# Preparing a last attention layer early, during another layer's context steps, and keeping it in DRAM

## The chip, the cores and the metric

The kernel runs on one core of a Trainium2 chip. A core has TensorE (PE, with its weight loads PEld), VectorE (DVE), ScalarE (ACT), GpSimd (POOL) and SyncE (SP, which here only issues DMAs), each with a queue of its own that is worked off in order. Data lie in SBUF (128 partitions) and PSUM, and in DRAM. The metric is the device time of one execution in microseconds (us), as the median of several runs.

## The reference

Four transformer blocks in a row change `x` (8 batch elements, 256 tokens, 320 channels, float32), with a context of 120 rows by 192 channels per batch element:

- Layer 0: self-attention, cross-attention to the context, both with 20 heads and with queries, keys, values and softmax weights rounded to 8-bit steps, then a gated feed-forward.
- Layer 1: self-attention, cross-attention, gated feed-forward, unquantised.
- Layer 2: cross-attention to 104 text rows and 16 image rows, each with keys and values of its own.
- Layer 3, 8 heads, the layer that the change is about:

```python
enc, ca = encoder_hidden_states[:, :end_pos], encoder_hidden_states[:, end_pos:]   # 116 rows, 4 tokens
hs = _mha(hidden_states @ Wq, enc @ Wk, enc @ Wv)
ca_q1 = jnp.einsum('btc,th->bch', ca, Wq_ca)[:, indices, :]
ca_hs1 = _mha(ca_q1, residual, residual)
ca_hs2 = _mha(ca_hs1 @ Wq, ca @ Wk_ca, ca @ Wv_ca)
out = (hs + ca_hs2) @ Wout + b_out + residual
```

Three products in it depend on the context and the weights alone, not on `x`: `Wq_ca` spread over heads (`wz`), the token keys `ca @ Wk_ca` behind `Wq` (`wk2`), and the token values `ca @ Wv_ca` before `Wout` (`v2W`). Making these three is "the preparation".

## The kernel before, in words

`x` stays in SBUF throughout. The program text fixes the order of the work: Python generators yield after each piece, and two helpers interleave them.

- `weave(*parts)` runs rounds. In each round it takes one piece from every part whose start round has come. `paced(steps, idle)` makes a part give a piece only every `idle + 1` rounds.
- `run_flow(items)` runs layer 0's feed-forward and everything after it as a pipeline of items. An item has four generators: `project`, `tops` (row maxima of the scores), `out` (exponentials, values, output) and `fin`. In step `i` it takes turns among `tops` of item `i+1`, `project` of `i+2`, `fin` of `i-1` and `out` of `i`. Items 0 to 3 are layer 0's feed-forward, 4 to 11 and 12 to 19 layer 1's two attentions, 20 to 23 its feed-forward, then layer 2's eight attention items ("both") and layer 3's eight (`last_item`).

Layer 0's second attention (class `Quant`, object `c`) has two weaves. The first, the score loop, combines `tops_all` (scores and their maxima, L1309 and L1312), `sums_all` (exponentials L1360 and their sums L1375), the rounding of the operands (`whole_all`) and the values (`v`). It takes six rounds per batch element. The second, the output loop, is `out_all`: exponentials again, rounded weights (DVE, L1468), values (L1450), output projection (`project_out_steps`). It takes three rounds per batch element, 24, and four to drain.

Both weaves also carry `context_steps`: 29 pieces that compute the keys and values of the context for layers 1, 2 and 3 (matmuls L668 and L670), evict them with ACT into staging tiles (`kst`, one buffer; `vst`, two) and write them with SP's DMAs to DRAM, where the later items fetch them. One piece is taken ahead; 18 run in the score loop, one in three rounds; the other 10 in the output loop, one in two rounds. The staging and the context's weights lie in the pool `context`, on the right side of SBUF. When it closes, the pool of layer 0's second feed-forward weights (`w_ff2`) takes its place; the load of `ff2` (L96) waits for that.

`load_last` runs after step 23. It closes the feed-forward pools, opens `w_last` in their place and issues the loads of layer 2's output weights (40 DMAs, L275) and layer 3's weights: `lwk_ca`, `lwv_ca` (L96, L98), `lwq` (L776), `lwo` (L790), then `open_last` (L795 to L853). That one loads `sel` and `wq_ca`, fills `wz` and `ones`, and returns an item of its own, inserted at place 29 among layer 2's items:

- its `project`, `first`: three transposes of `wq_ca` (L815), multiplied by a head mask into `wz` (L817, L821); then `k2` and `v2T`, the token keys and values spread by head (12 matmuls each, L120, and three multiplications, L834);
- its `tops`, `second`: `wk2` = `WqT` times `k2` (18 matmuls, copies L845, L846) and `v2W` = `v2T` times `Wout` (12 matmuls, copy L851);
- its `out` and `fin` are empty.

`WqT` and `Wout` for it come through the pool `f_weights`, tag `o`, two buffers. SP issues DMAs in the program's order, so the small DMAs of `top_scores` that carry the row maxima `nT` into `qT` (L397) wait behind whatever SP was given earlier. `out` of the same item cannot start its score matmuls (L414) before these have landed. Layer 3's `last_item` reads `wz` and `wk2` in `project` (L890, L127) and `v2W` in `fin`.

Of the kernel before, what the change touches and what calls it, by code (L numbers as in the profile page):

```python
# [11 lines left out]
F32 = mybir.dt.float32  # L12
BF16 = mybir.dt.bfloat16
AF = mybir.ActivationFunctionType
ALU = mybir.AluOpType
# [3 lines left out]
P = 128  # L19
# [19 lines left out]
T3 = 4  # L39
# [15 lines left out]
class Kernel:  # L55
# [737 lines left out]
    def open_last(self, pool, w):  # L793

        nc = self.nc  # L795
        HT = H3 * T3
        w["pool"] = pool
        sel = w["sel"] = pool.tile([Q3, 2, N], F32, name="sel3")
        nc.sync.dma_start(sel, self.a["sel"].rearrange("(t p) n -> p t n", p=Q3))
        wq_ca = pool.tile([T3, C], F32, name="wq_ca")  # L800
        nc.sync.dma_start(wq_ca, self.a["L3_xattn_Wq_ca"])
        wz = w["z"] = pool.tile([P, 3, H3, PAD], F32, name="wz")
        nc.gpsimd.memset(wz, 0.0)
        ones = w["ones"] = pool.tile([P, PAD3], F32, name="ones3")
        nc.gpsimd.memset(ones, 1.0)
        k2, v2T = (self.work.tile([P, 3, B * HT], F32, tag="xh", name=n) for n in ("k2", "v2T"))
        wk2 = w["k2"] = pool.tile([P, 3, B * HT], F32, name="wk2")
        v2W = w["v2"] = pool.tile([P, B * HT // P, C], F32, name="v2W")
        pairs = lambda m: self.cols[:, COL_BMK + m * HT : COL_BMK + (m + 1) * HT]

        def first():

            ps = self.bank()
            for c, n in CH:
                nc.tensor.transpose(ps[:n, c * T3 : (c + 1) * T3], wq_ca[:, c * P : c * P + n], self.ident[:T3, :T3])  # L815
            for c, n in CH:
                nc.vector.tensor_tensor(  # L817
                    wz[:n, c, :, :T3], pairs(c)[:n].rearrange("p (h t) -> p h t", t=T3),
                    ps[:n, c * T3 : (c + 1) * T3].unsqueeze(1).to_broadcast([n, H3, T3]), ALU.mult,
                )  # L820
            nc.scalar.copy(wz[64:, 2], wz[:64, 2])  # L821
            yield

            rep = [self.ctxT[:n, c, :, K3:].unsqueeze(2).to_broadcast([n, B, H3, T3]) for c, n in CHC]
            for dst, wt in ((k2, w["wk_ca"]), (v2T, w["wv_ca"])):
                yield
                ps = self.pair()
                for m, rows in CH:
                    o = ps[:rows, m // 2, m % 2 * B * HT : (m % 2 + 1) * B * HT]
                    self.mm(  # L830
                        o.rearrange("p (b h t) -> p b h t", h=H3, t=T3),
                        [(wt[:n, c, m * P : m * P + rows], rep[c]) for c, n in CHC],
                    )
                    nc.vector.tensor_tensor(  # L834
                        dst[:rows, m].rearrange("p (b k) -> p b k", k=HT), o.rearrange("p (b k) -> p b k", k=HT),
                        pairs(m)[:rows].unsqueeze(1).to_broadcast([rows, B, HT]), ALU.mult,
                    )

        def second():

            ps = self.pair()
            for m, rows in CH:
                o = ps[:rows, m // 2, m % 2 * B * HT : (m % 2 + 1) * B * HT]
                self.mm(o, [(w["wqT"][:n, c, m * P : m * P + rows], k2[:n, c]) for c, n in CH])
                nc.scalar.copy(wk2[:rows, m, :], o)  # L845
            nc.scalar.copy(wk2[64:, 2, :], wk2[:64, 2, :])  # L846
            yield
            ps = self.pair()
            for i in range(B * HT // P):
                self.mm(ps[:, i, :C], [(v2T[:n, c, i * P : (i + 1) * P], w["wo_rows"][:n, c, :]) for c, n in CH])  # L850
            nc.scalar.copy(v2W, ps[:, :, :C])  # L851

        return first, second, lambda: iter(()), lambda: iter(())  # L853
# [652 lines left out]
def kernel(ctx: ExitStack, tc: tile.TileContext, a, out):  # L1506
    k = Kernel(ctx, tc, a, out)
    with ExitStack() as es:
# [15 lines left out]
        with tc.tile_pool(name="l0", bufs=1) as pool:  # L1524
# [17 lines left out]
            with tc.tile_pool(name="context", bufs=1, side="right") as cp:  # L1542
                k.open_context(cp, dram)
                ahead = k.context_steps()
                next(ahead)
                loaded["w"] = [k.weight_ff1(fp, "L0_xattn_Wff1")]
                brow["ff0"] = k.bias_row(k.fk, 2)
                w["self"], brow["self"] = load("L1", "q1", "k1", "v1", "o1_w", 3)
                c.steps()
                for _ in c.whole(0, True):  # L1550
                    pass
                n = len(c.units)
                k.weave(
                    (0, c.tops_all()), (n + 4, c.sums_all()), (0, c.whole_all()), (5, v),
                    (1, k.paced(islice(ahead, 18), 2)),
                )
                c.weight_steps()
                k.weave((0, c.out_all()), (0, k.paced(ahead, 1)))
# [16 lines left out]
        def load_last():  # L1575
# [3 lines left out]
            w3.update({f"w{n}": k.weight(pool, f"lw{n}", f"L3_xattn_W{n}") for n in ("k_ca", "v_ca")})  # L1579
            w3["wqT"] = k.weight(k.fw, "o", "L3_xattn_WqT", 2)  # L1580
# [93 lines left out]
```

## Time and profile before

| | us |
|---|---|
| median of 3 runs | 2303.44 |
| lowest, highest | 2302.2, 2305.42 |
| the profiled execution's own time | 2306.57 |
| span of its profile | 2304.7 |
| score loop of layer 0's second attention, about | 447 to 566 |
| its output loop, about | 585 to 691 |
| first and last matmul of the preparation's `first` and `second` | 1857.3 and 1902.6 |
| first matmul that reads `lwq` (layer 3's first item) | 1967.0 |

The profiled execution is one run with a hardware profiler; its own time is 1.87 us more than its span (what lies ahead of the first and behind the last instruction). Times in the text are counted from the start of that span. Where a line of the profile is labelled L120, it is the helper `mm`, whatever the matmul is for, and tiles tell these apart: the profile calls `wk2` and `k2` without their digits, `wk` and `k`, and the `WqT` and `Wout` tiles `o`. A row of the chain of waits gives its start, its length, and the engine, tile and line, with the number of instructions merged.

### The profile page before, as it was taken

Reading aid. Unit: us, or ns where it says so; the run is one execution under the profiler, and the core shown is the slowest. Engines: PE = TensorE matmul, PEld = TensorE weight load, DVE = VectorE, ACT = ScalarE, POOL = GpSimd, SP = SyncE. Lnnn points to the kernel's source line nnn. Section 1 sums busy time; section 2 is a strip of 40 time slices with the busy share of each in tenths; the row PEclk is TensorE's granted clock in tenths of the full one; section 3 lists DMA queues with packets and bytes.
Section 4 is the critical chain, followed back from the end, with each engine's and each line's share of the span. In section 5 each row is a group of like instructions: output and inputs, shape, how many; then the busy total and the mean of one; then the engine's idle time right before and its main releaser. Section 6 shows DMA issues by size and latency. Waiting matters only on the chain.

```text
span 2304.7 us, 38236 instructions
## 1 busy us (share of the span) xinstructions
PE 2104.4 (91%) x16413; PEld 1187.8 (52%) x16413; DVE 1117.6 (48%) x1691; ACT 823.0 (36%) x1248; POOL 360.3 (16%) x371
## 2 busy tenths in 40 slices
PE   7978878789789999999999999999999798999997
PEld 4643344544454455465555555454455455566664
DVE  4288666454761222236565666511122555555465
ACT  2347866357542121124444433310212222222221
POOL 1093055450520000000000010100001000001100
PEclk9989888799799999999999999999999899999999
DMA  4010000432220000020001101100000200000000
GB/s 113 14 14 2 1 1 1 116 104 65 54 74 4 0 1 0 1 89 2 2 2 27 38 24 41 34 1 0 1 1 14 54 24 13 19 21 23 26 17 17
DMA packets 78439, 60.99 MB, mean 26 GB/s; under 512 B 48314, under 2 KB 68222, under 8 KB 77758
## 3 DMA queue, kind: packets, MB, share of 16 engines
q1 hardware_dynamic: 74206, 54.83, 8.7%
q10 hardware_dynamic: 4064, 3.71, 0.5%
q8 instruction: 130, 2.13, 0.4%
q14 instruction: 39, 0.32, 0.0%
HBM read 41.49 MB, written 16.25 MB: 25 GB/s over the span
## 4 chain that ended last, share of the span: by engine, by line
PE 72%; DVE 15%; ACT 5%; issue 3%; POOL 2%; SPq 2%; DMA 1%; ACTq 0%; DVEq 0%; POOLq 0%
PE pf L564 13%; PE pf L120 12%; PE pf L127 9%; PE pa L120 7%; PE pa L431 6%; PE pf L414 4%; PE pf L568 4%; PE pf L129 3%; DVE negm L1312 3%; PE pf L369 2%; DVE rs L439 2%; PE pf L1353 2%; PE pa L1375 2%; PE pf L668 2%; DVE negm L376 2%
## 5 line engine op out<-in xcount | busy, mean ns | idle before, releaser
L564 PE MATMUL pf<-xTf,ff 128*128 128x512 f32 x640 | 294.9, 603 | 3.7 <-DVE negm L376 2.5
L420 ACT ACTIVATE e<-pf 128x1024 f32<-128x1024 f32 (+2 forms) x176 | 157.6, 944 | 231.5 <-PE pf L414 225.0
L376 DVE TENSOR_REDUCE negm<-pf 128x4 f32<-128x1024 f32 (+4 forms) x224 | 187.8, 885 | 104.4 <-PE pf L369 104.4
L439 DVE RECIPROCAL rs<-pa 128x256 f32<-128x256 f32 x88 | 152.3, 1745 | 143.9 <-PE pa L431 143.9
L573 DVE SCALAR_TENSOR_TENSOR hT<-pf,cols_sb,gl 128x512 f32<-128x512 f32 x80 | 60.1, 751 | 331.2 <-ACT gl L572 331.2
L564 PEld LDWEIGHTS pf<-xTf,ff 128*128 128x128 f32 x640 | 115.1, 190 | 161.8 <-issue 154.9
L461 POOL TENSOR_TENSOR xb<-x_sb,brow 128x640 f32<-128x640 f32 x40 | 62.0, 1550 | 825.9 <-DVE x_sb L467 782.2
L1360 ACT ACTIVATE e<-pf,sc_s 128x1024 f32<-128x1024 f32 x160 | 169.4, 1116 | 54.9 <-PE pf L1353 48.8
L1312 DVE TENSOR_REDUCE negm<-pf 128x4 f32<-128x1024 f32 (+2 forms) x128 | 143.4, 1132 | 64.6 <-PE pf L1309 58.3
L120 PE MATMUL pf<-ff,hT 128*128 128x320 f32 x640 | 174.4, 434 | 0.0
L572 ACT ACTIVATE gl<-pf,cols_sb 128x512 f32<-128x512 f32 x80 | 55.0, 687 | 305.0 <-PE pf L568 305.0
L414 PE MATMUL pf<-qT,kT 32*128 32x256 f32 (+1 forms) x1280 | 129.4, 415 | 24.6 <-DMA qT<-nT 16.0
L120 PEld LDWEIGHTS pf<-ff,hT 128*128 128x128 f32 x640 | 120.9, 190 | 55.5 <-issue 6.1
L369 PE MATMUL pf<-kT,qT 32*128 32x120 f32 (+1 forms) x1920 | 114.6, 334 | 17.3 <-ACT e L420 17.1
L120 PE MATMUL pa<-o,oT 128*128 128x320 f32 x352 | 109.8, 454 | 10.1 <-DVE oT L440 8.9
L369 PEld LDWEIGHTS pf<-kT,qT 32*128 32x128 f32 x1920 | 85.1, 194 | 55.2 <-ACT e L420 25.8
L581 POOL TENSOR_TENSOR xb<-x_sb,brow 128x640 f32<-128x640 f32 x16 | 25.1, 1570 | 559.4 <-DVE x_sb L586 543.8
L431 PE MATMUL pa<-e,v 128*32 128x256 f32 (+1 forms) x1280 | 108.4, 394 | 3.1 <-ACT e L420 1.7
L1353 PE MATMUL pf<-Q,K 32*128 32x256 bf16 (+1 forms) x960 | 86.7, 300 | 25.8 <-DVE negm L1312 17.6
L414 PEld LDWEIGHTS pf<-qT,kT 32*128 32x128 f32 (+1 forms) x1280 | 72.1, 185 | 73.2 <-issue 42.1
L1468 DVE TENSOR_SCALAR w<-e 128x1024 bf16<-128x1024 f32 (+2 forms) x128 | 87.1, 689 | 46.6 <-ACT e L1360 46.3
L127 PE MATMUL pf<-xT,q 128*128 128x256 f32 x384 | 102.3, 396 | 2.1 <-DVE hT L573 1.9
(279 smaller groups left out, 3371.3 us busy)
## 6 DMA issues: line engine op xcount, KB each, us to landing
ff<-in_L_xattn_Wff_dram SPq DMA_DIRECT2D x1, 2560.0 KB
qT<-nT SPq DMA_DIRECT2D x160, 4.0 KB
ff<-in_L_xattn_ff_w_dram SPq DMA_DIRECT2D x1, 2560.0 KB
out_dram<-x_sb SPq DMA_DIRECT2D x16, 160.0 KB
kd_cross<-kst SPq DMA_DIRECT2D x8, 300.0 KB
vd_cross<-vst SPq DMA_DIRECT2D x8, 300.0 KB
vd_both<-vst SPq DMA_DIRECT2D x8, 300.0 KB
kT<-kd_cross SPq DMA_DIRECT2D x8, 300.0 KB
```

Source lines behind the costliest of these rows:

```text
L120: self.nc.tensor.matmul(out, l, r, start=i == 0, stop=i == len(pairs) - 1)
L127: self.nc.tensor.matmul(o, *t[c], start=c == 0, stop=False)
L369: nc.tensor.matmul(s[j // 2][:, j % 2, o : o + nk], qT[r : r + PAD, g, t * P : (t + 1) * P], kT[r : r + PAD, g, :nk], start=True, stop=True,)
L376: nc.vector.tensor_reduce(negm[:, n, 2 * i : 2 * i + 2, g0 : g0 + len(gs), :].rearrange("p j g t -> p j (g t)"), sv[:, :, :, k0:k1], AX.X, ...
L414: nc.tensor.matmul(s[j // 2][:ks, j % 2, o : o + N], kT[r : r + PAD, g, c * ks : (c + 1) * ks], qT[r : r + PAD, g, :], start=True, stop=True,)
L420: nc.scalar.activation(e[:ks, 2 * i : 2 * i + 2, :n], s[i][:ks, :, :n], AF.Exp, scale=scale)
L431: nc.tensor.matmul(o[j * PAD : (j + 1) * PAD, what * N : (what + 1) * N], w, es[g][:ks, j, c * N : (c + 1) * N], start=first and c == 0 an ...
L439: nc.vector.reciprocal(rs, o[:, N:])
L564: nc.tensor.matmul(s[:, k, :], w1[:, c, col : col + P], xT[:, c, :], start=c == 0, stop=False)
L1312: nc.vector.tensor_reduce(negm[:, 2 * h : 2 * h + 2, gs[0] : gs[-1] + 1, :].rearrange("p j g t -> p j (g t)"), s[:, :, : len(gs) * TPB * n ...
L1353: nc.tensor.matmul(s[at // 2][:ks, at % 2, o : o + N], l, m, start=not shift and o == 0, stop=shift and o + N == n, skip_group_check=True,)
L1360: nc.scalar.activation(e[:ks, :, :n], ps[:ks, :, :n], AF.Exp, scale=self.sc[:ks, 9:10])
```

## The change

The preparation becomes a generator, `weights_last_steps`, that runs behind the last context step in the output loop. It has a pool of its own (`ahead_last`, opened where `context` was closed), loads its weights there, and writes `wz`, `wk2` and `v2W` to three DRAM tiles (384, 384 and 320 KB) from a staging tile. It yields five times with work between: `wz`, `k2`, `wk2`, `v2T`, `v2W`. The zero fill of `wz` is an ACT instruction there, in place of POOL's memset. `open_last` now loads the three from DRAM. The item at place 29 is gone, and so are the loads of `lwk_ca`, `lwv_ca`, `WqT` and `Wout` in `load_last`. The context steps are moved forward: 21 run in the score loop, one in two rounds, and the remaining 7 with the preparation in the output loop, again one in two rounds.

```diff
     def open_last(self, pool, w):
...
+        w["k2"] = pool.tile([P, 3, B * HT], F32, name="wk2")
+        w["v2"] = pool.tile([P, B * HT // P, C], F32, name="v2W")
+        w["z"] = pool.tile([P, 3, H3, PAD], F32, name="wz")
+        for n in ("z", "k2", "v2"):
+            nc.sync.dma_start(w[n], self.wd[n])
         sel = w["sel"] = pool.tile([Q3, 2, N], F32, name="sel3")
...
+    def weights_last_steps(self, pool, dram):
+        nc = self.nc
+        HT = H3 * T3
+        self.wd = {"z": dram.tile([P, 3, H3, PAD], F32, name="wd_z"),
+                   "k2": dram.tile([P, 3, B * HT], F32, name="wd_k2"),
+                   "v2": dram.tile([P, B * HT // P, C], F32, name="wd_v2")}
+        wq_ca = pool.tile([T3, C], F32, name="wq_ca")
+        nc.sync.dma_start(wq_ca, self.a["L3_xattn_Wq_ca"])
+        wca = {n: self.weight(pool, f"w{n}", f"L3_xattn_W{n}") for n in ("k_ca", "v_ca")}
+        big = lambda n: self.weight(pool, "big", n)
+        wt = big("L3_xattn_WqT")
+        staged = lambda n: pool.tile([P, 3, B * HT], F32, tag="staged", name=n)
+        heads = lambda n: pool.tile([P, 3, B * HT], F32, tag="heads", name=n)
...
+        wz = staged("wz_st").rearrange("p c (h r) -> p c h r", r=PAD)
+        zero = self.ident[:, :1].unsqueeze(2).to_broadcast([P, 3 * H3, PAD])
+        nc.scalar.activation(wz.rearrange("p c h r -> p (c h) r"), zero, AF.Identity, scale=0.0)
+        ps = self.pair()
...
+        nc.scalar.copy(wz[64:, 2], wz[:64, 2])
+        nc.sync.dma_start(self.wd["z"], wz)
+        yield
+        k2 = by_head(heads("k2"), wca["k_ca"])
+        yield
+        ps = self.pair()
+        st = staged("wk2_st")
+        for m, rows in CH:
+            o = ps[:rows, m // 2, m % 2 * B * HT : (m % 2 + 1) * B * HT]
+            self.mm(o, [(wt[:n, c, m * P : m * P + rows], k2[:n, c]) for c, n in CH])
+            nc.scalar.copy(st[:rows, m, :], o)
+        nc.scalar.copy(st[64:, 2, :], st[:64, 2, :])
+        nc.sync.dma_start(self.wd["k2"], st)
+        wt = big("L3_xattn_Wout")
+        yield
+        v2T = by_head(heads("v2T"), wca["v_ca"])
+        yield
+        ps = self.pair()
+        for i in range(B * HT // P):
+            self.mm(ps[:, i, :C], [(v2T[:n, c, i * P : (i + 1) * P], wt[:n, c, :]) for c, n in CH])
...
+        nc.scalar.copy(st, ps[:, :, :C])
+        nc.sync.dma_start(self.wd["v2"], st)
+        yield
...
-                    (1, k.paced(islice(ahead, 18), 2)),
+                (1, k.paced(islice(ahead, 21), 1)),
...
-                k.weave((0, c.out_all()), (0, k.paced(ahead, 1)))
+            def rest():
+                yield from ahead
+                context.close()
+                with tc.tile_pool(name="ahead_last", bufs=1, side="right") as pool:
+                    yield from k.weights_last_steps(pool, dram)
+
+            k.weave((0, c.out_all()), (0, k.paced(rest(), 1)))
...
-            w3.update({f"w{n}": k.weight(pool, f"lw{n}", f"L3_xattn_W{n}") for n in ("k_ca", "v_ca")})
-            w3["wqT"] = k.weight(k.fw, "o", "L3_xattn_WqT", 2)
-            w3["wo_rows"] = k.weight(k.fw, "o", "L3_xattn_Wout", 2)
...
-            w3["item"] = k.open_last(pool, w3)
+            k.open_last(pool, w3)
...
-        items.insert(29, lambda: w3["item"])
```

`by_head` holds the former matmuls and mask products of `k2` and `v2T` unchanged.

## The prediction

> **What bounds the kernel now.** I read the page first: TensorE is busy almost throughout and carries most of the chain that ended last, so an instruction taken off it counts unless something else is late behind it.
>
> ```profile
> span 2304.7 us, 38236 instructions
> ...
> PE 2104.4 (91%) x16413; PEld 1187.8 (52%) x16413; DVE 1117.6 (48%) x1691; ACT 823.0 (36%) x1248; POOL 360.3 (16%) x371
> ...
> PEclk9989888799799999999999999999999899999999
> ...
> PE 72%; DVE 15%; ACT 5%; issue 3%; POOL 2%; SPq 2%; DMA 1%; ACTq 0%; DVEq 0%; POOLq 0%
> ```
>
> To be seen: 91% busy, a granted clock that sags in places, 72% of the chain on PE. An average says nothing of a stage, so next come the two stages that the change touches. The late one is the run of steps in which layer 2's items meet the preparation item. I cut it where PE resumes `out` of a new item (first L414 of a step).
>
> ```profile
> core 0: us, PE busy (x) PEld busy (x) DVE busy (x) ACT busy (x) POOL busy (x), PEclk, DMA share, GB/s
> 1808.26:1834.28 26.02, 24.15 (x242) 15.26 (x242) 16.16 (x22) 8.41 (x14) 0.00 (x0) 0.84 0.17 48
> 1834.28:1864.18 29.90, 27.02 (x251) 16.16 (x251) 17.50 (x27) 7.60 (x12) 1.54 (x1) 0.89 0.11 28
> 1864.18:1897.51 33.33, 32.02 (x242) 16.86 (x242) 17.06 (x26) 8.48 (x15) 2.60 (x4) 1.00 0.07 21
> 1897.51:1938.27 40.76, 35.36 (x327) 21.74 (x327) 20.71 (x30) 11.63 (x21) 4.10 (x5) 1.00 0.06 17
> 1938.27:1963.66 25.39, 23.33 (x242) 14.52 (x242) 16.17 (x22) 8.41 (x14) 0.00 (x0) 0.87 0.06 17
> ```
>
> The columns are stretch, length, busy time of PE, PEld, DVE, ACT and POOL, then the granted clock and the DMA's share and GB/s. The first and the last row are ordinary steps: 26.02 and 25.39 us, mean 25.7. The three between are 29.90, 33.33 and 40.76 us, and PE is busy in nearly all of it. The last holds two steps, the second without any `out`. The chain of waits there:
>
> ```profile
> 1933.67 0.82 PE pf L314 x6
> ...
> 1936.44 1.58 DMA qT<-nT
> 1938.02 0.25 issue
> 1938.27 1.14 PE pf L414 x14
> ```
>
> PE finishes the next transposes at 1934.49 and does nothing until 1938.27, because the row maxima (`nT`) must still go through a DMA into `qT`, and no `out` covers that.
>
> The early stage is layer 0's second attention. It has two loops: the score loop (447 to 566 us, PE busy 106.2 of 119.0) and the output loop (585 to 691, PE busy 90.1 of 106.0). I cut them by batch element, by the times of DVE's L1312 and L1468:
>
> ```profile
> 536.90:549.20 12.30, 11.36 (x144) 5.64 (x145) 7.14 (x14) 8.36 (x14) 0.00 (x0) 1.00 0.20 51
> 644.00:660.70 16.70, 14.44 (x111) 8.86 (x110) 7.54 (x16) 8.25 (x14) 2.62 (x2) 0.95 0.15 57
> 660.70:671.90 11.20, 10.09 (x87) 6.08 (x85) 8.01 (x16) 6.77 (x10) 2.24 (x2) 1.00 0.17 50
> 671.90:680.30 8.40, 6.58 (x71) 3.75 (x70) 7.15 (x16) 5.39 (x6) 2.71 (x2) 0.98 0.56 190
> ```
>
> The first row is one batch element of the score loop with two context steps: PE 11.36 of 12.30 us. The other three are the output loop with two, one and no context step: 16.7, 11.2 and 8.4 us. So one context step of 3.2 us of PE (L668 and L670, 0.98+0.62+0.98+0.62 in the chain at 656 to 658) lengthens the loop by 2.8 to 4.15 us. These loops hide little PE work.
>
> **What is removed late.** PE's work of the preparation, from the chain: `k2` 1.25+1.25+1.15 = 3.65, `v2T` 1.26+1.25+1.15 = 3.66, `wk2` 1.69+1.63+1.58 = 4.90, `v2W` 4.01, three transposes 0.29; together 16.5 us. Its evictions (ACT 0.37x3, 0.40x2, 0.69; DVE 0.4x6, 0.18x3) lie beside PE. Its slot in the pipeline goes too: the step with no `out`. The five intervals sum to 155.4 us; five ordinary ones are 5 x 25.7 = 128.5. Gain **26.9**, of which 16.5 is work, 3.8 the wait on `nT`, and the rest (6.6) other gaps and the ten L120 matmuls at 1858.55 that take 5.63 us where ten take 2.89 elsewhere. Next late after this is the ordinary step itself; layer 3's items need `wz`, `wk2`, `v2W` over 100 us after they are loaded.
>
> **SP's queue in `load_last`.** PE idles 11.89 us until 1808.26 for `nT`, which SP issues from 1803.33 after all the weights; so each issue ahead of it is on the path. Removed: four `lwk_ca`/`lwv_ca` loads (1787.41 to 1789.65, 2.24 us) and `wq_ca` (0.44). Added: three loads from DRAM, each like `kT<-kd_both` (0.39 plus a gap of 0.1), 1.5 us. Net -1.2. Against it stands a rule: the Trainium skill, "DMA: Bandwidth & Descriptors", section on queues, rings and completion order, says that each DMA engine consumes a ring's descriptors in order. The three loads are 1.09 MB and stand right ahead of `nT`; at the 426 GB/s that the trace shows for `ff` at 984 to 988 us they take 2.6 us. If `nT` waits for all of it, the sum is +1.4; by the issue times alone -1.2. Part of the data moves while SP still issues, so I take **-0.5**, and keep -1.2 to +1.4. WqT and Wout leave SP at 1308.8 and 1480.2; the `nT` behind them were issued at 1319 or later anyway: nothing. The POOL memset of `wz` (0.74) precedes nothing urgent: nothing. If that cover failed it would cost its 0.74.
>
> **What is added early.** All of the preparation's PE work, 16.5 us, now stands among the last rounds of the output loop, one piece every second round; the context moves forward to make room: three steps (values of batch 7, L2's image keys, L3's first values) leave the output loop for the score loop. From the chain these are 1.27+0.73 = 2.0, 1.15+0.73+0.72+0.72 = 3.3 and 1.83+0.75 = 2.6: 7.9 us.
> - Output loop: +16.5 -7.9 = **+8.6**, at an exposure of 1 (2.8 to 4.15 for 3.2 in the rows above, i.e. 0.88 to 1.3). The fill of `wz_st` has no row; ACT's L744 fills 192 columns in 0.36 and L1360 moves 1024 in 1.1, so 768 lie between, about 0.9; ACT is busy about half of this loop (54.2 of 106), so nothing. If uncovered: 0.9 plus 2.6 of other evictions. The first load into the new pool must await the last context tiles' writes, then land; the transposes come two rounds (about 7 us) later, against a write of 4.5 and a load of some 2: nothing, at worst 2. The write-backs and `ff2`'s load shift by up to 20 us; `ff2` was issued at 670 and is first used at 740: nothing.
> - Score loop: +7.9 at PE's 92 to 96% busy. Also, a context step now comes every second round instead of every third. Each writes a staging tile that the next may not touch until its DMA has landed: `kst` has one buffer, `vst` two.
>
> ```profile
> 569.55 0.95 ACT vst L721 x2
> 570.51 0.02 issue
> 570.52 4.51 DMA vd_both<-vst
> ```
>
> This is such a wait: ACT may write `vst` again only 4.51 us after the last write's end. The rule: the same page, section "Anatomy of one DMA", puts a fixed part of about 2 us, mostly the receipt of the write, on top of bytes over 436 GB/s (fitted there to GpSimd's queue, while SP issues these); for 300 KB an estimate of 2.7 us. The trace says 4.51, and decides. At two rounds PE has 2.73 (a third of 8.2, an element's PE time without context steps: 12.3 less 2 x 2.0) plus 2.0 for values or 3.0 for keys: 4.8 or 5.7 us. The buffer's cycle is about 0.8+4.51+0.1 = 5.4 for the cross values, 2.3 of ACT (507.24 to 509.5) plus some 4 = 6.3 for keys. Excess 0.6 x 4 and 0.6 x 7, i.e. 6.6 by the row. By the rule the cycles are 3.6 and 5.0, and the excess is nil. With three PSUM pairs PE can run a little ahead of a waiting ACT. I take half the row, **+3.5**, between 0 and 10. Behind ACT's wait stand the `e` exponentials (L1360), and behind those PE's L1375 sums.
>
> **Sum.** -26.9 -0.5 +8.6 +7.9 +3.5 = **-7.4 us**. Against the profiled execution (2306.57 us, of which the span is 2304.7) that is 2299.2; it lies 3.1 above the median of the timed runs, 2303.44, so I forecast **2296.0**.
>
> **Rivals.**
> 1. *The loops hide it.* PE is idle 12.8 us in the score loop and 15.9 in the output loop; if half of the 24.4 us of moved and added work fell into it, early cost would be 20.0 - 12.2 = 7.8, total -19.6, 2283.8. For: the idle time is there, and the output loop's elements differ from 8.4 to 16.7 us. Against: the three rows above, where each step shows in full.
> 2. *It only changes place.* The dense pacing costs the full 10 instead of 3.5: total -0.9, 2302.5. For: ACT evicts `kst` on the chain already. Against: between values steps of L2 the two `vst` take turns, 9.6 us apart.
> 3. *Slower, by the staging buffers and the clock.* If each of the 21 dense steps waits 1.5 us and PE, idle in those waits, drops to half its clock (granted 0.50 from 448 to 460 us after a gap at 444 to 449, 0.59 from 585 to 605), the score loop pays 21 x 1.5 = 31.5 instead of 3.5: total +20.6, 2324. It turns slower, by more than a measurement tells from no change, from 3.5+7.4+4.6 = 15.5 us, 0.74 a step. Against: PE's share of 92 to 96% leaves it little idle.
> 4. *It doesn't do what it says:* the DRAM loads land late and the empty slot remains as a wait on `nT`. Then the 3.8 us of waiting and some 2 of other gaps stay: 2302. The order of instructions speaks against it: `nT` of every item is now followed by an `out`. It is counted with 2.
>
> **Chances.** The forecast's case 0.55, its own range 2290 to 2301; rival 1 0.22; rivals 2 and 4 0.13; rival 3 0.10. A measurement here tells about 0.2% (4.6 us) from no change. Faster: 0.46 of the 0.55 and rival 1, 0.68; within 0.2%: 0.09 and 0.13, 0.22; slower 0.10. The range 2285 to 2305 leaves out rival 3 and the far half of rival 1, and takes in the bounds of the staging wait (0 to 10) and of the three loads.
>
> **What would show it.** Between the item before and `out` of the next, all intervals from 1808 on should be 25 to 26 us; no matmul of the preparation after 720 us; PE's wait before 1808 should be 11 to 13 us long. The score loop should grow by about 11 us (8 to 18), with waits of ACT on `kst` or `vst` DMAs in the list; the output loop by about 9. I am wrong if the output loop grows by more than 15 (the new pool's first loads late), if ACT's waits on staging exceed 10 us, or if the late steps keep a gap of several us before L414.

## The result and the profile after

| | kernel before | changed kernel |
|---|---|---|
| time, median (us) | 2303.66 (2302.2 to 2305.42, 4 executions) | 2281.80 (2280.65 to 2286.03, 4 executions) |
| profiled execution: span, own time | 2304.7, 2306.57 | 2280.5, 2282.32 |
| its mean granted clock | 0.956 | 0.964 |

The ratio is 0.9908, with a 95% interval of 0.9893 to 0.9924: 21.9 us less. The forecast was 7.4 less, 2296.0, with a range from 2285 to 2305. The direction was right; the time lies outside the range, near rival 1 (2283.8).

The same lines of the page as were read before, now of the changed kernel:

```profile
span 2280.5 us, 38243 instructions
...
PE 2090.2 (92%) x16413; PEld 1181.9 (52%) x16413; DVE 1116.1 (49%) x1691; ACT 824.9 (36%) x1249; POOL 359.0 (16%) x370
...
PEclk9979888899899999999999999999999899999999
...
PE 73%; DVE 15%; ACT 4%; issue 3%; POOL 2%; SPq 2%; DMA 1%; ACTq 0%; DVEq 0%; POOLq 0%
```

PE has the same 16413 matmuls and is busy 14.2 us less. No matmul was removed, so the difference lies in how long they took: at which clock they ran, and how well they followed each other.

The late steps, cut at the first L414 of each item, with the columns as in the prediction (stretch, length, busy time of PE, PEld, DVE, ACT, POOL, granted clock, DMA share, GB/s):

```profile
1809.28:1836.00 26.72, 24.85 (x239) 15.77 (x239) 16.16 (x22) 8.42 (x14) 0.00 (x0) 0.81 0.17 51
1836.00:1861.95 25.95, 23.88 (x250) 14.86 (x249) 17.22 (x24) 8.41 (x14) 1.54 (x1) 1.00 0.09 26
1861.95:1887.90 25.95, 23.88 (x250) 14.85 (x249) 17.22 (x24) 8.42 (x14) 1.54 (x1) 1.00 0.09 27
1887.90:1913.85 25.95, 23.88 (x250) 14.86 (x249) 17.22 (x24) 8.41 (x14) 1.54 (x1) 1.00 0.09 26
1913.85:1939.80 25.95, 23.88 (x250) 14.86 (x249) 17.21 (x24) 8.42 (x14) 1.54 (x1) 1.00 0.06 17
```

All are ordinary steps now; the intervals of 29.90, 33.33 and 40.76 are gone. The five sum to 130.5 us after 155.4, which is 24.9 less (forecast 26.9: an ordinary step is 26.1 us here, not 25.7).

The early stage is cut at four marks that exist in every kernel: the start of the score loop (DVE's step size), the first element's sums, the fifth element's sums, the loop's end, and the first matmul of the feed-forward. So the four rows are the first element's stretch, elements 1 to 4, elements 5 to 7 with the tail, and the output loop. Of the kernel before:

```profile
445.54:497.47 51.93, 40.71 (x324) 21.43 (x325) 29.76 (x50) 22.15 (x57) 44.15 (x36) 0.80 0.40 113
497.47:550.91 53.44, 50.55 (x568) 26.24 (x568) 28.05 (x49) 37.19 (x69) 0.00 (x0) 1.00 0.35 87
550.91:581.10 30.19, 28.56 (x294) 12.96 (x293) 8.73 (x24) 22.94 (x33) 0.00 (x0) 1.00 0.17 45
581.10:692.69 111.59, 92.17 (x696) 53.30 (x695) 81.67 (x171) 58.10 (x86) 46.85 (x58) 0.86 0.23 67
```

And of the changed kernel:

```profile
445.13:498.66 53.53, 44.89 (x349) 24.77 (x350) 28.51 (x49) 24.95 (x69) 44.23 (x36) 0.87 0.50 142
498.66:558.18 59.52, 55.25 (x606) 28.68 (x605) 28.84 (x50) 41.09 (x73) 0.00 (x0) 1.00 0.40 93
558.18:579.92 21.74, 21.05 (x262) 9.47 (x261) 8.74 (x24) 18.94 (x24) 0.00 (x0) 1.00 0.14 34
579.92:697.85 117.93, 100.12 (x724) 55.65 (x724) 85.36 (x180) 58.73 (x85) 46.11 (x58) 0.91 0.21 68
```

The score loop takes 134.8 us after 135.6, with three more steps in it: +1.6, +6.1 and -8.5. Counted by their L668 groups, the first stretch has 9 steps instead of 6, elements 1 to 4 have 12 instead of 8, and the last three elements none instead of 4. The output loop grows by 6.3.

Where the 24.2 us between the two spans went, by the same marks and the feed-forwards' stores:

| stage | before | after | change | forecast |
|---|---|---|---|---|
| up to the score loop | 445.5 | 445.1 | -0.4 | 0 |
| score loop | 135.6 | 134.8 | -0.8 | +11.4 |
| output loop | 111.6 | 117.9 | +6.3 | +8.6 |
| from there to the first store of layer 1's feed-forward | 840.6 | 837.4 | -3.2 | 0 |
| from there to its last store | 234.1 | 234.1 | 0 | 0 |
| the rest (load_last, layers 2 and 3) | 537.4 | 511.2 | -26.2 | -27.4 |

The gap to the forecast is thus 12.2 in the score loop, 3.2 in a stage that the change doesn't touch, 2.3 in the output loop and 0.4 ahead of the loops, less 1.2 late. These are two single executions; c1, below, shows how much of it another execution repeats.

### The profile page after: what moved, and what is told of

Read it like the earlier page. It is cut to its first block, busy times and chain, and to the rows that moved or that the text cites. A ratio compares the mean times of both kernels' runs of the same rounds, so it can differ in the third digit from the quotient of the medians.

```text
span 2280.5 us, 38243 instructions
## 1 busy us (share of the span) xinstructions
PE 2090.2 (92%) x16413; PEld 1181.9 (52%) x16413; DVE 1116.1 (49%) x1691; ACT 824.9 (36%) x1249; POOL 359.0 (16%) x370
## 4 chain that ended last, share of the span: by engine, by line
PE 73%; DVE 15%; ACT 4%; issue 3%; POOL 2%; SPq 2%; DMA 1%; ACTq 0%; DVEq 0%; POOLq 0%
PE pf L564 13%; PE pf L120 12%; PE pf L127 9%; PE pa L120 6%; PE pa L431 6%; PE pf L414 4%; PE pf L568 4%; PE pf L129 3%; DVE negm L1335 3%; PE pf L1376 2%; DVE rs L439 2%; PE pf L369 2%; PE pa L1398 2%; DVE negm L376 2%; DVE rs L1054 2%
## 5 line engine op out<-in xcount | busy, mean ns | idle before, releaser
L1335 DVE TENSOR_REDUCE negm<-pf 128x4 f32<-128x1024 f32 (+2 forms) x128 | 143.3, 1133 | 65.9 <-PE pf L1332 59.4
L414 PE MATMUL pf<-qT,kT 32*128 32x256 f32 (+1 forms) x1280 | 128.1, 412 | 17.0 <-DMA qT<-nT 8.6
L414 PEld LDWEIGHTS pf<-qT,kT 32*128 32x128 f32 (+1 forms) x1280 | 72.0, 183 | 64.3 <-issue 32.2
```

What stands on the lines that cost most here:

```text
L414: nc.tensor.matmul(s[j // 2][:ks, j % 2, o : o + N], kT[r : r + PAD, g, c * ks : (c + 1) * ks], qT[r : r + PAD, g, :], start=True, stop=True,)
L1335: nc.vector.tensor_reduce(negm[:, 2 * h : 2 * h + 2, gs[0] : gs[-1] + 1, :].rearrange("p j g t -> p j (g t)"), s[:, :, : len(gs) * TPB * n ...
```

## The experiments

Three theories. **A**, the forecast's: both loops are bound by PE, so a step costs its PE time wherever it is put, and the staging buffers add 3.5 us. **B**: the score loop has waits (on DVE's row maxima, on POOL's rounding) that hide steps. **C**, formed on the way: steps cost their PE time, but at the clock that is granted, and the denser order draws a better clock. "Half-clock time" below is (1 - granted clock) x 2 x length: an estimate that takes each stretch for a mixture of the two values 0.50 and 1.00, which finely cut stretches show (last rows of this part).

### The late half alone: e9 and e4

e9, the kernel before with the preparation left out altogether (the outputs of the preparation are zeros):

```diff
-            w3["item"] = k.open_last(pool, w3)
+            k.open_last(pool, w3)
...
-        items.insert(29, lambda: w3["item"])
```

> The kernel before without the preparation: its item, its four weights' loads and all of its instructions are left out, wk2, v2W and wz stay zero, and the output is not the reference's. This is the late half of the change with no early price. Prediction: -26.9 in the late steps, -0.5 to -2 in the loads, so 2274 to 2277. If the late slot was partly clock: -20 to -23, some 2280.

Measured 2275.39 (2275.25 to 2278.22) beside 2302.12: -26.7, ratio 0.9883 (0.9866 to 0.9900). The forecast's late terms (-27.4) hold.

e4, the preparation late, but without a slot:

```diff
-        items.insert(29, lambda: w3["item"])
...
+        def joined(make):
+            p, t, o, f = make()
+            first, second = w3["item"][:2]
+            return lambda: chain(p(), first()), lambda: chain(t(), second()), o, f
...
+        items[29] = lambda make=items[29]: joined(make)
```

> The kernel before with the preparation's two parts run behind the projection and behind the tops of layer 2's item 5, late as before, but with no slot of its own in the pipeline. If the slot cost what the prediction says (the wait on nT 3.8 and other gaps 6.6 beside 16.5 of work): -10 us, some 2293. If the work is the whole cost: 0, 2303. If the work alone hides beside other items: -20 or more.

Measured 2292.36 beside 2302.18, -9.8, ratio 0.9952 (0.9935 to 0.9969). So the split was right too: the slot cost about 10; the rest of e9's 26.7, about 17, is the work.

With e9 the price of the early half can be read from medians: the changed kernel lies 2284.68 - 2275.39 = 9.3 above it (2284.68 is c1's median, below). The forecast had 20.0.

### Density and steps apart: e1, e11, e10

e1 changes the pacing alone:

```diff
-                    (1, k.paced(islice(ahead, 18), 2)),
+                    (1, k.paced(islice(ahead, 21), 1)),
```

> The kernel before with the denser pacing alone (21 context steps, one every second round, in the score loop); the preparation stays late. Theory A (the prediction's: the score loop is bound by PE, so a moved step costs its PE time, and staging adds 3.5): score loop +11.4 us, output loop -7.9, total +3.5, some 2307. Theory B (the first 45 us of the score loop wait for the row maxima on DVE and run in part at half clock, and moved steps fill those waits): score loop -2 to +2, output loop -6 to -9, total -5 to -10, some 2296. The late stage is as before in both.

Measured 2300.78 (2293.73 to 2317.46) beside 2302.18, ratio 1.0002 (0.9982 to 1.0023): unclear between the two. Its profile is that of its fastest execution:

```profile
443.26:496.79 53.53, 44.90 (x349) 24.79 (x350) 28.49 (x50) 24.96 (x69) 44.23 (x36) 0.87 0.50 142
496.79:556.46 59.67, 55.25 (x606) 28.67 (x605) 28.82 (x50) 41.08 (x73) 0.00 (x0) 1.00 0.40 92
556.46:578.21 21.75, 21.06 (x262) 9.47 (x261) 8.75 (x25) 18.95 (x24) 0.00 (x0) 1.00 0.14 34
578.21:687.83 109.62, 88.15 (x667) 50.65 (x667) 81.97 (x171) 55.14 (x78) 47.48 (x58) 0.86 0.15 51
```

The score loop is 134.95 us, as in the changed kernel, but the output loop is only 2.0 shorter than before, 109.6. Both theories missed that.

e11 keeps the 18 steps and takes only the denser pacing (`islice(ahead, 18), 1`):

> The kernel before with its 18 context steps of the score loop one every second round instead of every third: only the density changes, no step leaves the output loop. Reading of the traces so far: in the first five batch elements seven more steps cost 7.7 us (1.1 each), in the last three elements four fewer give back 8.5 (2.1 each). By that the score loop shrinks by 5 to 8 us against the kernel before (18 steps end by element 4, and the three moved steps are not there), to 127 to 130, and the three moved steps cost 5 to 8 of it back in the changed kernel: the denser order pays for them. If instead the loop hides the three steps themselves: 134 to 135, as with 21. Theory A's staging waits: +3.5, 139.

```profile
445.67:499.16 53.49, 44.86 (x349) 24.73 (x350) 28.35 (x49) 24.96 (x69) 44.23 (x36) 0.87 0.50 142
499.16:551.73 52.57, 49.30 (x578) 25.50 (x577) 28.61 (x50) 37.99 (x66) 0.00 (x0) 1.00 0.34 81
551.73:573.42 21.69, 21.06 (x262) 9.50 (x261) 8.74 (x24) 18.76 (x24) 0.00 (x0) 1.00 0.01 2
573.42:686.66 113.24, 93.68 (x696) 54.14 (x695) 81.66 (x171) 58.16 (x86) 46.91 (x58) 0.85 0.23 66
```

This is e11's profile. Its score loop is 127.75 us, so beside the kernel before (135.6) **the density gives -7.9 in these two profiles**. The three steps that e1 adds at the same density cost 134.95 - 127.75 = **+7.2**. Their matmuls (L668 and L670) take 6.5 us in that loop; the forecast's 7.9 had been read in the output loop, two of the three steps at a granted clock of 0.50. So the loop doesn't hide the steps (theory B): their cost is paid, and here the density pays it back. The forecast's price of the density had the wrong sign.

That holds for one state of the clock only. With the old pacing the score loop is 135.6, 135.2 (e10), 134.4 (e9) and 134.2 us (e4), each time with a first stretch of 51.8 to 51.9 us at 0.80. The dense profiles fall apart: the first stretch has 0.87 in the changed kernel, e1, e8 and e11, and 0.80 to 0.83 in c1, e2 and e5, where the loop is longer (141.8 to 146.7, with 21 steps). In the median e11 is 2297.66 beside 2301.13, ratio 0.9988 (0.9972 to 1.0004): 3.5 less, in an interval that includes no gain.

e10 is the changed kernel with the old pacing (18 steps, one in three rounds; ten and the preparation in the output loop):

> The changed kernel with the old pacing: 18 context steps in the score loop, one every third round, and the other ten with the preparation's six pieces in the output loop. Theory A (each step costs its PE time in either loop): score loop -11.4, output loop +7.9 against the changed kernel, total -3.5. Theory B (the score loop takes the three steps for nothing): score loop -1 to +1, output loop +2 to +6 (the pacing alone moved it by 2.0), total +2 to +6.

Measured 2293.66 (2292.7 to 2294.4), ratio 0.9955 (0.9936 to 0.9974): 9.0 above the changed kernel's 2284.68, more than either theory said.

```profile
445.14:496.94 51.80, 40.38 (x324) 21.41 (x325) 30.02 (x50) 22.18 (x57) 44.21 (x36) 0.80 0.40 113
496.94:550.40 53.46, 50.55 (x568) 26.25 (x568) 28.06 (x50) 37.24 (x69) 0.00 (x0) 1.00 0.35 87
550.40:580.38 29.98, 28.57 (x294) 12.96 (x293) 8.73 (x24) 22.96 (x33) 0.00 (x0) 1.00 0.17 46
580.38:706.46 126.08, 107.72 (x753) 60.51 (x752) 86.86 (x186) 61.68 (x93) 47.00 (x63) 0.89 0.23 67
```

The score loop is 135.2, level with the changed kernel's 134.8; the output loop is longer, 126.1 after 117.9. The output loop of e9 has the same context steps but no preparation:

```profile
579.09:692.74 113.65, 94.79 (x696) 54.77 (x695) 81.88 (x171) 58.16 (x86) 46.77 (x58) 0.82 0.23 66
```

Between the two, 16.5 us of PE work lengthen the loop by 12.4. From e10 to the changed kernel (117.9, and 118.4 in c1) the three steps give back 8.2 or 7.7, full price. Without the preparation they give back less: the loop with ten steps is 111.6 (before), 113.2 (e11), 113.7 (e9) and 114.1 us (e4), with seven 109.6 (e1), which is 2.0 to 4.5. A loop with less work in it has more room.

### The preparation in the output loop: e2

The changed kernel with `k2`, `v2T`, `wk2` and `v2W` left out; zeros are staged and written:

```diff
-        k2 = by_head(heads("k2"), wca["k_ca"])
         yield
...
-            self.mm(o, [(wt[:n, c, m * P : m * P + rows], k2[:n, c]) for c, n in CH])
...
+        nc.scalar.activation(st.rearrange("p c (h r) -> p (c h) r", r=PAD), zero, AF.Identity, scale=0.0)
```

> The changed kernel without the preparation's k2, wk2, v2T and v2W matmuls and their evictions; zeros are staged and written in their place, so the output is not the reference's. Theory A (the output loop shows PE work in full): -16.2 us against the changed kernel (3.65+3.66+4.90+4.01), some 2266. If the loop hides half of it: -8, some 2274. The score loop and the late stage stay as in the changed kernel.

Measured 2277.19 (2269.46 to 2292.79), ratio 0.9902 (0.9869 to 0.9934): 7.5 below c1. Its output loop, in the profile of its slowest execution:

```profile
590.73:701.58 110.85, 89.37 (x670) 50.83 (x670) 82.13 (x174) 57.65 (x82) 47.48 (x58) 0.85 0.22 72
```

That is 110.9 after c1's 118.4. About half of the preparation's 16.2 us is hidden there, as rival 1 had it; from e1 to the changed kernel (109.6 to 117.9) it is about half as well.

### Is the first stretch held by POOL or DVE? e3, e5, e12, e13, e14

e3 starts the steps in round 15 (`(15, k.paced(islice(ahead, 21), 1))`):

> The changed kernel with the context steps starting in round 15 of the score loop instead of round 1, so that none lies in its first 40 us. Theory A (PE-bound throughout): the PE work is the same, so the score loop changes by -2 to +2 us. Theory B (the first stretch waits for DVE and POOL, and steps fill it): the first stretch stays nearly as long (down by less than half of the 18 us of PE work that leave it) and the later elements grow by about 18, so +9 to +18 us, some 2294.

The score loop is 141.9: +7.1 against the changed kernel's profile, but level with c1's 141.8 below. The first stretch falls to 37.9 us, 15.6 less, when some seven of its nine steps and 16.9 us of PE's busy time leave it. So it did not hide them. Median 2295.71, ratio 0.9975 (0.9958 to 0.9993).

e5 gives DVE the rounding of every second element (`self.whole(b, b % 2 == 1)`):

> The changed kernel with the rounding of batch elements 1, 3, 5 and 7 (all but its first instruction) on DVE instead of POOL; the same values are computed. Theory B in the form that POOL's 44 us of rounding hold the first elements: the first stretch shortens, score loop -4 to -10 us. In the form that the row maxima on DVE hold it (DVE's instructions being longer beside POOL's): DVE gets about 10 us more work, but POOL's disturbance halves: -3 to +4. Theory A (PE-bound): -1 to +1.

POOL's busy time falls from 44.2 to 23.8 us, and the first stretch is 62.3 us at a clock of 0.81, not shorter than c1's 59.4 at 0.80; the loop takes 146.7. DVE is busy 4.6 us longer in that stretch than in c1, and PE's waits for its maxima (`negm`) grow from 4.8 to 8.5 us, so the run exchanges one possible holder for another. But no wait of PE on POOL stands in the lists of either kernel's first stretch: POOL, busy without a gap for its first 44 us, is not seen to hold anything. Nor are the maxima longer beside a busy POOL: in the changed kernel they (128x960) take 1155 ns both from 447 to 490 us and from 495 to 548, where POOL is idle. Median 2302.91, ratio 1.0007 (0.9996 to 1.0019).

e12 leaves the steps out of the score loop:

> The kernel before with no context step in the score loop; all of them run in and behind the output loop, so only the score loop's length is of use. Theory A (full price): the 18 steps are some 45 us of PE, 135 - 45 = 90 us. If the first element's stretch waits for DVE and POOL: 36 to 38 us to the first sums instead of 52, and the loop 100 to 110.

```profile
445.36:482.61 37.25, 25.86 (x267) 13.22 (x269) 29.91 (x50) 13.22 (x21) 36.71 (x31) 0.66 0.19 55
482.61:519.38 36.77, 33.77 (x489) 15.96 (x490) 27.95 (x50) 23.82 (x31) 7.45 (x6) 0.78 0.01 2
519.38:544.02 24.64, 23.77 (x269) 10.42 (x263) 8.84 (x24) 18.79 (x23) 0.00 (x0) 0.80 0.01 2
```

The bare loop is 98.7 us, between A's 90 and B's 100 to 110; the first stretch is within B's 36 to 38, but e13 and c1 show that steps put there are paid. Its clock is only 0.74 over the loop: PE with less to do is at half clock about half of the time. With 18 dense steps (127.7) the clock is 0.95. The 18 steps thus cost 29 us, 1.6 each, although their PE time is some 2.5 (45 us, the estimate of the expectation). PE's busy time rises by only 31.8 us (83.4 to 115.2): the other matmuls take less time when the steps stand between them. That is theory C's first sign. (A single execution, 2334.7, since the steps then trail behind the output loop.)

e13 packs the first 12 steps one a round; e14 adds three more:

```diff
-                (1, k.paced(islice(ahead, 21), 1)),
+                (1, chain(k.paced(islice(ahead, 12), 0), k.paced(islice(ahead, 9), 1))),
```

> The changed kernel with the first 12 of the 21 context steps one in every round and the other 9 one in every second, so that more of them lie in the first element's stretch. If that stretch goes on hiding steps (three more cost it 1.6 us from the old to the new pacing): score loop -3 to -7 us, some 2280. If the staging buffers hold such dense steps (the forecast's theory of waits, at one round a step): waits of ACT on kst or vst of 5 to 12 us in the first stretch, score loop +3 to +10. If the stretch is full of PE work at nine steps: -1 to +1.

> As the run before with three more steps in the score loop (24 in all, the last at its element 4 or 5), so the output loop has four context steps and the preparation. If the first stretch hides steps: score loop -1 to +4 and output loop -3 to -8 against the changed kernel, some 2278. If the steps cost their full price there: score loop +5 to +8, output loop -3 to -8, no gain. If the writes of vd_last hold ACT as in the run with 24 evenly paced steps (10.3 us of waits): score loop +10 or more.

In e13 the first stretch holds 15 steps instead of 9 and takes 72.6 us at a clock of 0.88: +19.0 for six, 3.2 each, with PE busy 17.2 longer; full price. ACT waits 7.0 us for writes of `vst` and 3.3 for `kst`: the forecast's staging waits, but only at one step a round. Score loop 140.0, median 2300.56, ratio 0.9980 (0.9969 to 0.9991). e14: score loop 158.5, output loop 115.0, 2303.04, ratio 0.9988 (0.9975 to 1.0001). No better version came of it.

### 24 steps, evenly: e8

> The changed kernel with 24 context steps in the score loop instead of 21, so three more steps (L3's values and keys) leave the output loop. Theory A (every step costs its PE time in either loop): 0 to +3 against the changed kernel. Theory B (the score loop takes more at little cost): the output loop gives back 6 to 8 us; the score loop's last elements have no other step, so they take part of it: -3 to -7, some 2277.

`islice(ahead, 24), 1`. Measured 2294.57 (2289.24 to 2306.7), ratio 0.9979 (0.9963 to 0.9994). The output loop is 115.0, but the score loop 151.9. ACT's and PE's waits in it:

```profile
ACT vst L745 <- DMA vd_last<-vst: 10.3, 4, 4.3
```

```profile
PE pf L1332 <- ACT vst L745: 4.5, 1, 4.5
...
PE pt L1343 <- ACT sums L1403: 2.9, 1, 2.9
```

The columns are total, times and longest, in us. Here the wait that the forecast priced does stand: ACT holds at `vst` for up to 4.3 us (the prediction's row had 4.51), and PE behind it. It comes with the 22nd to 24th step, which write `vd_last` one after another, just past where the change stops. In the changed kernel the only wait on such a write among ACT's longest is the next line (the kernel before had 1.2 us of it), and behind PE's waits there stands none:

```profile
ACT vst L744 <- DMA vd_both<-vst: 3.4, 2, 3.2
```

### The clock: c1, e6, e7

c1 is the changed kernel, unaltered:

> The changed kernel once more, unaltered, with many executions, because executions of one kernel differ by the time that the granted clock spends at 0.5. Across the executions of the kernel before, each us at half clock goes with 0.27 to 0.33 us of time; its mean clock is 0.956, and that of the four executions behind the result 0.964. If the gain of 21.9 is the change's own: mean clock 0.963 to 0.965, median 2279 to 2286. If it was partly a good draw of the clock: mean clock 0.958 to 0.962, median 2286 to 2294, and at equal time at half clock some 8 us below the kernel before.

Nine executions: median 2284.68 (2279.77 to 2304.24) beside 2302.12, ratio 0.9927 (0.9903 to 0.9951), mean clock 0.962. The median lies in the first expectation's range, the clock in the second's. The change is worth 17 to 22 us; its four first executions, at 0.963 to 0.965, drew well. Means tell how much goes with the clock: 2286.5 us with 173 us at half clock here, 2303.5 with 200 in the 15 executions of the kernel before. A straight line through those 15 has 0.28 us of time for each us at half clock, one through these nine 0.44. By these, 8 to 12 of the 17 us go with the clock, and 5 to 9 would remain at equal half-clock time: an estimate, and what goes together need not be the cause.

The profile of c1 (2290.9 us), of the same instructions as the changed kernel's:

```profile
446.35:505.72 59.37, 49.47 (x349) 26.82 (x350) 30.81 (x49) 25.07 (x69) 44.20 (x36) 0.80 0.45 128
505.72:566.42 60.70, 56.89 (x606) 29.33 (x605) 28.82 (x49) 41.09 (x73) 0.00 (x0) 0.97 0.41 92
566.42:588.17 21.75, 21.06 (x264) 9.47 (x261) 8.75 (x24) 18.94 (x24) 0.00 (x0) 1.00 0.10 30
588.17:706.58 118.41, 100.36 (x725) 55.86 (x724) 85.35 (x180) 58.73 (x85) 46.10 (x58) 0.91 0.21 68
```

The first stretch takes 59.37 instead of 53.53 us at a clock of 0.80 instead of 0.87, and the loop 141.8. At 0.80, the clock that the kernel before has there, three more steps cost 59.37 - 51.93 = 7.4, for 8.8 us more of PE's busy time. In this state nothing is left of the density's gain: 141.8 less the 7.2 of the three moved steps is 134.6, within the 134.2 to 135.6 of the old pacing (an estimate; no profile has 18 dense steps in this state). The first stretch of c1, cut further:

```profile
450.00:461.00 11.00, 9.73 (x53) 5.47 (x54) 4.44 (x4) 2.38 (x6) 11.00 (x9) 0.50 0.43 126
461.00:505.72 44.72, 39.74 (x297) 21.36 (x297) 23.16 (x36) 21.53 (x59) 30.10 (x25) 0.87 0.44 123
```

Behind the same gap the changed kernel is back at 0.99 from 460 us on (row below); here the mean stays at 0.87. Over five profiles with these 21 steps, the score loop goes with its half-clock time: 134.8 and 135.0 us with 13.7 (changed kernel, e1), 141.9 with 23.9 (e3), 141.8 with 27.3 (c1), 145.8 with 37.5 (e2). Other edits leave that line: e6 and e7, below, have 134.8 and 136.8 us with only some 7 and 10, and e5, with more work on DVE, 146.7 with some 30. The output loop goes with it too: 117.9 and 118.4 with 20.5, 127.1 with 37.5 (e13, same instructions there).

e6 adds 12 matmuls that nothing reads in PE's gap ahead of the score loop; e7 adds 6 more ahead of the output loop:

```diff
+    def idle_work(self, n):
+        ps = self.pair()
+        for i in range(n):
+            self.nc.tensor.matmul(
+                ps[:, i % 2, :256], self.ident, self.x[:, i % 2, :256], start=True, stop=True
+            )
...
             c.steps()
+            k.idle_work(12)
```

> The changed kernel with 12 matmuls more, whose result nothing reads, in PE's gap of 3.9 us at the head of the score loop (445 to 449 us). After that gap PE's granted clock is 0.50 until about 460. If the clock falls because PE was idle: it stays near 1.0 and the score loop shortens by 3 to 6 us (11 us at half clock, in which PE is busy 9.8). If the clock falls for another reason: 0 to +2.

> As the run with 12 idle matmuls at the head of the score loop, and 6 more at the head of the output loop (581 to 585 us, after which the granted clock is 0.50 to about 592). If idleness lowers the clock: 2 to 4 us less than with the first gap alone. If PE is delayed more by the added matmuls than the clock gives back: +1 to +2.

The gap and what follows it, first of the changed kernel, then of e6:

```profile
445.13:449.00 3.87, 0.17 (x8) 0.18 (x12) 3.21 (x9) 1.15 (x4) 3.33 (x4) 0.74 0.60 191
449.00:460.00 11.00, 9.77 (x54) 5.39 (x46) 4.44 (x4) 2.38 (x6) 11.00 (x10) 0.50 0.41 126
460.00:498.66 38.66, 34.95 (x297) 19.20 (x296) 20.86 (x36) 21.42 (x59) 29.91 (x24) 0.99 0.51 142
```

```profile
442.67:447.00 4.33, 4.33 (x28) 3.54 (x30) 3.21 (x9) 0.97 (x3) 3.79 (x4) 1.00 0.57 180
447.00:460.00 13.00, 11.03 (x89) 6.42 (x85) 9.13 (x13) 5.08 (x13) 13.00 (x12) 1.00 0.47 153
460.00:495.23 35.23, 30.63 (x261) 16.41 (x261) 18.90 (x29) 18.73 (x52) 27.37 (x22) 0.95 0.52 138
```

Filling the gap keeps the clock at 1.00 through 460, where it was 0.50. So PE's idleness does lower it, in this gap. But the first stretch shrinks only from 53.53 to 52.56, and both loops lose it again: the score loop is 134.8 and the output loop 127.9 (at 0.85). Medians: e6 2290.13 (2276.76 to 2301.5), ratio 0.9945 (0.9928 to 0.9963); e7 2290.63, ratio 0.9958 (0.9946 to 0.9970). Both are level with c1 within the intervals, or behind it. Why 11 us at full clock in place of half gain just 1 us there stays open. PE's waits on DVE's maxima are no longer than before (3.1 us after 3.5), so they are not what ate it; and the clock sags elsewhere, to 0.95 from 460 us on.

## Why the prediction was right in direction and wrong in size

1. **Late, -26.9 and load_last -0.5: right.** -26.2 by the profiles, -26.7 by e9. The slot's share (e4: -9.8) was right as well. From the feed-forward's last store to the first L414 the changed kernel takes 40.0 us after 40.9, so the loads gave -0.9, within the -1.2 to +1.4 and near the -1.2 of the issue times alone: `nT` did not wait for all of the three loads' bytes. Whether it stood behind them in a ring, no run here shows. PE's wait there fell from 11.89 to 8.24, below the 11 to 13 that I expected, but mostly because PE's own work before it ended later.
2. **Output loop, +8.6: right in the sum, by luck in the terms.** +6.3 and +6.8 in the two profiles at a clock of 0.91, and +15.5 in e13 at 0.85. The forecast was +16.5 and -7.9, each at an exposure of 1. Measured in the one order, preparation first, they are +12.4 (e10 over e9) and -7.7 (e10 to c1); in the other, -2.0 (before to e1) and +8.3 (e1 to the changed kernel). Too much was charged for what comes and too much credited for what goes, and the errors cancel. The exposure had been read by comparing elements of one loop; what removing a step gives back is another quantity.
3. **Score loop, three steps +7.9: right in size.** +7.2 at equal density (e11 to e1), for 6.5 us of PE time in that loop; the 7.9 had been read in part at half clock.
4. **Score loop, the denser pacing +3.5 "between 0 and 10": this is the step that failed.** It measured -7.9 in the profile (e11 beside before; -6.5 beside the shortest loop with the old pacing), -3.5 in e11's median, and by the estimate for c1's state about 0; nowhere +3.5. I gave it a lower bound of zero without a reason that excluded a gain. The staging waits were nil on PE's path at this density (they come at 24 steps, e8, or in ACT at one step a round, e13). And I did not ask what the old pacing cost: it ran four steps in the last three elements, where the rows show 30.19 us before and 21.7 without steps, 2.1 each; moved into the first five elements, seven steps (these four and the three) cost 7.7 in the changed kernel's profile, 1.1 each, but 14.7 in c1's, again 2.1 each. From before to e11 PE's busy time fell by 4.6 us (119.8 to 115.2) with the same matmuls, and its idle time by 3.2 (15.7 to 12.5). Half-clock time fell from 20.5 to 13.7 us; by the five loops with 21 steps, (145.8 - 134.8) / (37.5 - 13.7) = 0.46 us for each, the clock would be 3.1 of the 7.9. That is an estimate, and e6 and e7 do not lie on its line. So these profiles show that the gain goes with the clock; that the density causes the better clock is not shown.
5. **The clock as a rival only on one side.** Rival 3 let PE's waits halve the clock; that the clock could rise was not priced anywhere, and by the means of c1 it goes with 8 to 12 of the 17 us. Rival 1 came near the time, yet for a reason that holds in one loop only: the output loop hides half of the preparation (e2), the score loop hides none of the three steps.
6. **The middle, -3.2: not the change.** It stands at two places where the clock is 0.86 before and 1.00 after, in unchanged code. From layer 0's feed-forward to layer 1's, e4 and e9, with the old early stage, take 527.1 and 525.5 us, the kernel before 530.4, the changed one 527.2, and e2, with the new stage, 530.2. So the profile's 24.2 holds 3.2 us of luck.

What stays open: how often executions with the dense pacing draw the better state, and why. e11's median gained 3.5, and its interval includes zero; one profile each is no distribution.

## What to carry to other kernels

A change in the order of side work has a price and a return: count, per stretch of the loop, how many steps leave the places where they stood bare, not only what they cost where they go, and never bound such a term at zero. What the same steps cost depends on how full the loop already is (three steps: 2.0 to 4.5 us, or about 8 with the preparation beside them), so price the last one added, not the average. Before explaining a few us, look at the granted clock of both profiles in that stretch, and run the changed kernel once more.

## What the runs showed of the hardware

Executions of one kernel differed by more than expected: the kernel before by 2297.15 to 2312.7 in 34 executions, the changed one by 2279.8 to 2304.2 in nine, and both go with the granted clock. For the kernel before, whose clock of 0.956 means 2304.7 x 0.044 x 2 = 203 us at half clock, each such us goes with 0.27 to 0.33 us of time (straight lines through its executions in five sessions), so some 60 us, 2.6% of the span, by estimate. The Trainium skill, "TensorE: Matmul & The Clock Gate", Part 1, describes a gate that passes half or all of the clock by PE's recent activity, in a window that runs freely, so that its phase differs from run to run; the rows above (0.50 and 1.00, and 53.5 against 59.4 us for the same instructions) agree, though no run here shows the window itself. It puts the penalty of the ramp below 1% of a typical kernel's span. That is one ramp; here the clock falls again behind gaps within the kernel, and the estimate above is 2.6%.
